# The drain of a graph-attention layer kernel: which engine sums x for the held blocks, and in what order the last blocks are normalised

## The chip, the cores and the metric

The kernel runs on one core of one Trainium2 chip. The metric is device microseconds of one launch of the program; less is better.

## The reference

```python
def gat(h, adj_mat, W, a):                       # 4 heads, 512 wide; h is x, 4096 x 512; adj_mat 4096 x 4096
    ht  = (h @ W).reshape(N, 4, 512).transpose(1, 0, 2)
    src = einsum('hnd,hd->hn', ht, a[:, :512, 0]); dst = einsum('hnd,hd->hn', ht, a[:, 512:, 0])
    e   = leaky_relu(src[:, :, None] + dst[:, None, :], 0.01) + adj_mat[None]
    att = softmax(e, axis=-1)
    return einsum('hij,hjd->hid', att, ht).mean(axis=0)

out = layernorm(x + gat(x, adj, W, a), axis=-1)   # eps 1e-5, no scale or shift; all float32
```

The entries of adj go up to 1e9, so that in nearly every row one entry is larger than the next by so much that the softmax is 1 at that entry and 0 elsewhere. The attention of such a row is the projected row of x at the column of the row's largest entry.

## The kernel before

The function `leading_rows` computes the whole output on the assumption that each softmax has one winner, and counts the rows for which a bound does not prove this. The function `general` computes softmax in full for blocks with such rows; with these inputs it is branched over.

**Blocks.** The 4096 rows are 32 blocks of 128 (NB = 32); row p of block ib is row 32p + ib of the matrix. The names used below are Q = 4, BEHIND = 24 and LATE = 28. Blocks 24 to 31 are called the held blocks here: the loop does not add x to them in the first place that it does for the others.

**The loop over t = 0 to 31.** In each turn SP issues the load of block t + 5 of adj (2 MB; in four pieces for block 0 and blocks 28 to 31), through the queue q1. VectorE takes maxima of segments of 64 entries (L158), then the largest segment of each row (`find_segment`, L165, L167). GpSimd fetches that segment anew by an indirect DMA (`lead`, L171). Two turns later VectorE finds the place within the segment (`find_column`, L193), and GpSimd fetches the row of x at that column (`y`, L181) by another indirect DMA (`gather_rows`). One turn after that TensorE transposes y (`turn`, L208), ScalarE copies it out as `yt` (L210), and TensorE multiplies it by the mean of the heads' weights (`products`, L221; a float32 matmul of 128x512 is two records in the profile). For blocks below 24 the row's own x is added in PSUM by a product with the identity (`residual`, L214). ScalarE then computes mean and variance in two passes (`stats`, L243, L245), GpSimd the reciprocal root (`rstd`, L248 to L250), and ScalarE the normalised rows in place of x (`finish`, L254). For blocks 24 to 27 ScalarE only puts the projected rows by (`put_by`, L234), because their x is not loaded yet.

**The order.** The instructions of each engine are issued in the order of the program text (`manual_schedule`); the framework adds semaphores for dependencies. What is later in the text on an engine cannot overtake what is earlier. SP's DMAs have eight completion semaphores that are used in turn, so SP issues a DMA only when the eighth one before it has landed.

**The drain** is the text from the last turn of the loop on. SP loads x of the held blocks, then stores the first 24 blocks. For row block 31 VectorE searches the column in the whole row of adj (`find_column_in_row`, L201), without the fetch of the segment. `row_norm` (L228) is needed for the bound; `bound`, `test`, `count` and `report` compute the number of unproved rows, and on TensorE they are the small products `px` (L362, L367, L386), which stand between the turns and products of blocks 29 to 31. In the kernel before:

- x is added to the put-by rows of blocks 24, 25 and 26 by GpSimd (`add_x`, L237), the first of them ahead of the last segment fetch, the second and third around the fetch of y of block 31; block 27 is summed on VectorE. Blocks 28 and 29 get x by `residual` on TensorE.
- the last of the four products of blocks 24 to 28 stands behind the next block's `turn`.
- `moments`, `factor` and `normalise` are the pieces of a second kind of normalising, by `bn_stats` on VectorE with a root on ScalarE (L274, L278, L280, L283, L290). They are spread over the text, so that a root is asked for before its result is used. Blocks 27 to 31 use it; blocks 27 and 31 use ScalarE for the last step as well (`finish`, L303).
- block 31 is projected in two halves of 256 columns (L259, L263), each with its own statistics (`stats_of_half`, L297); in `finish_in_halves` VectorE writes one half and ScalarE the other.

SP stores blocks 28, 29, 24 with 25, 30, 26 with 27, and 31 at the end (L306).

Of the kernel before, what the change touches and what calls it, by code (L numbers as in the profile page):

```python
# [9 lines left out]
F32 = mybir.dt.float32  # L10
# [56 lines left out]
def leading_rows(ctx, tc, x, adj, W, a, out, ident, v, n_bad, any_bad):  # L67
# [47 lines left out]
    def load_x(lo, n):  # L115
        nc.sync.dma_start(hold[:, ds(lo, n), :], x_rows[:, ds(lo, n), :])
# [69 lines left out]
    def find_inner(ib):  # L186
        nc.vector.max(out=inner[:, ib, :], in_=lead_of[ib])
# [16 lines left out]
    def turn(ib):  # L204
        y = y_t.pop(ib)
        tp = psum.tile([P, KB, P], F32, name="tp", bufs=2)
        for kb in range(KB):
            nc.tensor.transpose(tp[:, kb, :], y[:, ts(kb, P)], ident)  # L208
        yt = yt_of[ib] = rows.tile([P, KB, P], F32, name="yt")
        nc.scalar.copy(yt, tp)  # L210

    def residual(ib):
        o_ps[ib] = psum.tile([P, D], F32, name="o")
        nc.tensor.matmul(o_ps[ib], ident, hold[:, ib, :], start=True, stop=False)  # L214

    def products(ib, lo=0, hi=KB):
        start = ib not in o_ps
        if start:
            o_ps[ib] = psum.tile([P, D], F32, name="o")
        for kb in range(lo, hi):  # L220
            nc.tensor.matmul(  # L221
                o_ps[ib], yt_of[ib][:, kb, :], w_sum[:, kb, :],
                start=(start and kb == 0), stop=(kb == KB - 1),
            )

    def row_norm(ib):
        sq = rows.tile([P, D], F32, name="sq")
        nc.scalar.activation(sq, hold[:, ib, :], AF.Square, accum_out=xx[:, ib : ib + 1])  # L228
# [4 lines left out]
            o_ps["by"] = adj_pool.tile([P, N // D, D], F32, name="adj_t")  # L233
        nc.scalar.copy(o_ps["by"][:, ib - BEHIND, :], o_ps.pop(ib))  # L234

    def add_x(engine, ib):
        engine.tensor_add(hold[:, ib, :], hold[:, ib, :], o_ps["by"][:, ib - BEHIND, :])  # L237
        o_ps[ib] = hold[:, ib, :]

    def stats(ib):  # L240
        o, i = o_ps[ib], slice(ib, ib + 1)
        sq = rows.tile([P, D], F32, name="sq")
        nc.scalar.activation(sq, o, AF.Identity, scale=-1.0 / D, accum_out=nm[:, i])  # L243
        sq = rows.tile([P, D], F32, name="sq")
        nc.scalar.activation(sq, o, AF.Square, bias=nm[:, i], accum_out=sd[:, i])  # L245

    def rstd(i):
        nc.gpsimd.tensor_scalar(sd[:, i], sd[:, i], 1.0 / D, EPS, op0=OP.mult, op1=OP.add)  # L248
        nc.gpsimd.tensor_tensor(sd[:, i], sd[:, i], power[:, : i.stop - i.start], op=OP.pow)  # L249
        nc.gpsimd.tensor_mul(nm[:, i], nm[:, i], sd[:, i])  # L250

    def finish(ib):
        i = slice(ib, ib + 1)
        nc.scalar.activation(hold[:, ib, :], o_ps.pop(ib), AF.Identity, bias=nm[:, i], scale=sd[:, i])  # L254

    def residual_in_halves(ib):
        o_ps[ib] = [psum.tile([P, D // 2], F32, name="o") for _ in range(2)]
        for k, o in enumerate(o_ps[ib]):
            nc.tensor.matmul(o, ident, hold[:, ib, ts(k, D // 2)], start=True, stop=False)  # L259
# [5 lines left out]
                start=False, stop=(kb == KB - 1),  # L265
            )

    mean_var, rt = {}, {}

    def moments(ib):  # L270

        if ib < NB - 1:
            st = small.tile([P, nc.vector.BN_STATS_DIM], F32, name="st", bufs=2)
            nc.vector.bn_stats(st, o_ps[ib])  # L274
        else:
            st = halves_st
        mv = mean_var[ib] = small.tile([P, nc.vector.BN_AGGR_DIM], F32, name="mv", bufs=3)
        nc.vector.bn_aggr(mv, st)  # L278
        r = rt[ib] = sd[:, ib : ib + 1]
        nc.scalar.activation(r, mv[:, 1:2], AF.Sqrt, bias=eps)  # L280

    def factor(ib, shift=False):
        nc.vector.reciprocal(rt[ib], rt[ib])  # L283
        if shift:
            nc.vector.scalar_tensor_tensor(
                nm[:, ib : ib + 1], mean_var[ib][:, 0:1], -1.0, rt[ib], op0=OP.mult, op1=OP.mult
            )

    def normalise(ib, o, columns=slice(0, D)):
        nc.vector.tensor_scalar(  # L290
            hold[:, ib, columns], o, mean_var[ib][:, 0:1], rt[ib], op0=OP.subtract, op1=OP.mult
        )

    halves_st = once.tile([P, 2, nc.vector.BN_STATS_DIM], F32, name="halves_st")

    def stats_of_half(ib, k):
        nc.vector.bn_stats(halves_st[:, k, :], o_ps[ib][k])  # L297

    def finish_in_halves(ib):

        halves, i = o_ps.pop(ib), slice(ib, ib + 1)
        normalise(ib, halves[0], slice(0, D // 2))
        nc.scalar.activation(hold[:, ib, D // 2 :], halves[1], AF.Identity, bias=nm[:, i], scale=sd[:, i])  # L303

    def store(queue, lo, n):
        queue.dma_start(out_rows[:, ds(lo, n), :], hold[:, ds(lo, n), :])  # L306
# [93 lines left out]
    for t in range(NB):  # L400
        if t == NB // 2:
            tc.mark_branch_hint_location("general", engines=HINTED)
        if t in x_at:
            load_x(*x_at[t])
        load_adj(t + AHEAD)
        middle = 1 if t > LATE else 2
        segment_maxima(t, 0, middle)
        if t >= COLUMN:
            find_column(t - COLUMN)
        segment_maxima(t, middle, PIECES)  # L410
        pair = FINISH <= t < BEHIND + FINISH and t % 2 == 0
        if pair:
            rstd(slice(t - FINISH, t - FINISH + 2))
        if t == NB - 1:
            for ib in (BEHIND, LATE, BEHIND + 2, LATE + 2):
                load_x(ib, 2)
            row_norm(BEHIND)
            row_norm(BEHIND + 1)
            add_x(nc.gpsimd, BEHIND)
        find_segment(t)  # L420
        if t < 2:
            mean_of_heads(t)
        elif t == 2:
            mean_of_heads(2)
            mean_of_heads(3)
        if t == 0:
            turn_a()
        turned = [(*vectors[0], turn_w(*vectors.pop(0))) for _ in range(vectors_at.get(t, 0))]
        if t == 16:
            head_norms()  # L430
        ib = t - PROJECT
        if ib >= 0:
            turn(ib)
            if ib > BEHIND:
                products(ib - 1, KB - 1, KB)
            if ib < BEHIND or ib == LATE:
                residual(ib)
        for some in turned:
            head_vector(*some)
        if ib >= 0:  # L440
            products(ib, 0, KB if ib < BEHIND else KB - 1)
        if t >= BEHIND + STATS:
            put_by(t - STATS)
        elif t >= STATS:
            stats(t - STATS)
            row_norm(t - STATS)
        if pair:
            finish(t - FINISH)
            finish(t - FINISH + 1)

    row_norm(BEHIND + 2)
    row_norm(BEHIND + 3)
    row_norm(LATE)
    store(nc.sync, 0, Q)
    for ib in range(Q, BEHIND, 2):
        store(nc.sync, ib, 2)
    find_column(NB - 2)
    add_x(nc.gpsimd, BEHIND + 1)
    find_column_in_row(NB - 1)
    add_x(nc.gpsimd, BEHIND + 2)  # L460
    turn(NB - 3)
    products(NB - 4, KB - 1, KB)
    residual(NB - 3)
    products(NB - 3)
    for ib in range(LATE + 1, NB):
        row_norm(ib)
    stats(BEHIND)
    moments(LATE)
    bound(0)
    for ib in range(BEHIND, NB):  # L470
        find_inner(ib)
    factor(LATE)
    normalise(LATE, o_ps.pop(LATE))
    turn(NB - 2)
    residual_in_halves(NB - 1)
    products(NB - 2, 0, 1)
    bound(1)
    add_x(nc.vector, LATE - 1)
    stats(BEHIND + 1)
    moments(LATE - 1)  # L480
    products(NB - 2, 1, KB - 1)
    rstd(slice(BEHIND, BEHIND + 2))
    stats(BEHIND + 2)
    bound(2)
    test()
    pg = count()
    rstd(slice(BEHIND + 2, BEHIND + 3))
    moments(NB - 3)
    factor(LATE - 1, shift=True)
    report(pg)  # L490
    factor(NB - 3)
    normalise(NB - 3, o_ps.pop(NB - 3))
    turn(NB - 1)
    finish(BEHIND)
    finish(BEHIND + 1)
    products(NB - 2, KB - 1, KB)
    products_of_half(NB - 1, 0)
    products_of_half(NB - 1, 1)
    nc.vector.tensor_add(hold[:, NB - 2, :], o_ps[NB - 2], hold[:, NB - 2, :])
    o_ps[NB - 2] = hold[:, NB - 2, :]  # L500
    moments(NB - 2)
    stats_of_half(NB - 1, 0)
    factor(NB - 2)
    normalise(NB - 2, o_ps.pop(NB - 2))
    finish(BEHIND + 2)
    finish(BEHIND + 3)
    stats_of_half(NB - 1, 1)
    moments(NB - 1)
    factor(NB - 1, shift=True)
    finish_in_halves(NB - 1)  # L510
    for ib, n in ((NB - 4, 1), (NB - 3, 1), (BEHIND, 2), (NB - 2, 1), (BEHIND + 2, 2)):
        store(nc.sync, ib, n)
    store(nc.sync, NB - 1, 1)


# [151 lines left out]
```

## Time and profile before

| what | before |
|---|---|
| median of 6 runs | 242.73 us (242.31 to 243.97) |
| the profiled execution's own time | 243.38 us |
| its span in the profile | 241.8 us, so 1.58 us lie around it |
| busy: TensorE, VectorE, ScalarE, GpSimd | 198.9, 186.7, 111.6, 101.2 us |
| moved by DMA | 97.73 MB, 404 GB/s on average |
| granted TensorE clock | 0.966 on average |

Times in the texts are microseconds from the start of the span of the profiled execution. PE is TensorE, DVE is VectorE, ACT is ScalarE, POOL is GpSimd, SP is SyncE; a q behind one of these names marks its instruction queue. In a line of the timeline the columns are the start, the duration, the engine, the source line, the operation, the output and inputs, shapes and the count, and in brackets how long the engine had been idle and what released it. In the lines that cut the span into 40 slices each digit is the busy share in tenths.

### The profile page before, as it was taken

What the parts mean: (1) busy time and instruction counts of PE and PEld (TensorE: products, weight loads), DVE (VectorE), ACT (ScalarE), POOL (GpSimd) and SP (SyncE); (2) the same over time, 40 slices, a digit from 0 to 9 for tenths busy, and PEclk for the clock granted to TensorE, in tenths of its full rate; (3) what the DMA queues carried; (4) which work ended last, traced back from release to release, by engine and by line L of the source; (5) the groups of instructions that cost most, each with busy time, mean ns of one, the idle gap of its engine ahead of it and who ended that gap; (6) DMA issues with size and microseconds to landing.
All of it is one profiled execution on the core that took longest, in us unless ns stands there. A gap on an engine that the chain in (4) does not pass through costs nothing.

```text
span 241.8 us, 2519 instructions
## 1 busy us (share of the span) xinstructions
PE 198.9 (82%) x683; PEld 102.4 (42%) x683; DVE 186.7 (77%) x308; ACT 111.6 (46%) x267; POOL 101.2 (42%) x215
## 2 busy tenths in 40 slices
PE   0097849899999999999968789688886988979891
PEld 0034516645555555555523334233333433334460
DVE  2617864659959895999599987998699999978592
ACT  2001202115575757575756464646464455247572
POOL 1022232405626463546434643564264554566130
PEclk9999799679999999999999999999997999999997
DMA  6999999999999999999999999999999999999985
GB/s 228 419 424 420 428 419 424 413 423 411 425 415 417 407 423 420 421 412 416 429 415 417 420 415 420 422 407 418 412 424 404 399 400 401 400 414 419 413 333 215
DMA packets 14850, 97.73 MB, mean 404 GB/s; under 512 B 2281, under 2 KB 2281, under 8 KB 9969
## 3 DMA queue, kind: packets, MB, share of 16 engines
q1 hardware_dynamic: 11232, 88.09, 88.4%
q0 software_dynamic: 3584, 9.44, 10.0%
q8 instruction: 6, 0.10, 0.2%
q14 instruction: 12, 0.09, 0.1%
q10 hardware_dynamic: 16, 0.02, 0.0%
HBM read 89.15 MB, written 8.39 MB: 403 GB/s over the span
## 4 chain that ended last, share of the span: by engine, by line
issue 31%; POOL 30%; DMA 23%; PE 10%; ACT 1%; DVE 1%; SPq 1%; POOLq 1%; DVEq 0%
DMA hold<-in_x_dram 13%; POOL y L181 10%; POOL lead L171 10%; PE o L221 5%; DMA hold<-in_L_gnn_W_dram 4%; POOL sd L249 4%; DMA y<-in_x_dram,col 3%; DMA lead<-in_adj_dram,row 2%; POOL start L176 2%; POOL row L169 2%; POOL col L195 2%; PE o L263 1%; PE o L214 1%; POOL sd L248 1%; PE pv L335 1%
## 5 line engine op out<-in xcount | busy, mean ns | idle before, releaser
L158 DVE TENSOR_REDUCE seg<-adj_t 128x32 f32<-128x2048 f32 (+1 forms) x74 | 146.3, 1987 | 40.2 <-DMA adj_t<-in_adj_dram 39.9
L221 PE MATMUL o<-w_sum,yt 128*128 128x512 f32 x248 | 117.5, 614 | 0.7 <-ACT yt L210 0.7
L221 PEld LDWEIGHTS o<-w_sum,yt 128*128 128x128 f32 x248 | 45.5, 195 | 54.9 <-issue 43.8
L210 ACT COPY yt<-tp 128x512 f32<-128x512 f32 x32 | 18.8, 587 | 44.2 <-PE tp L208 37.7
L171 POOL DMA_INDIRECT lead<-in_adj_dram,row x32 | 32.3, 1010 | 14.0 <-POOL row L169 14.0
L181 POOL DMA_INDIRECT y<-in_x_dram,col x32 | 30.9, 965 | 16.1 <-POOL col L195 14.6
L311 PE MATMUL o<-hold,ident 128*128 128x512 f32 x32 | 18.4, 727 | 17.7 <-DMA hold<-in_L_gnn_W_dram 17.7
L208 PE MATMUL tp<-ident,y 128*128 128x128 f32 x128 | 19.7, 277 | 15.2 <-DMA y<-in_x_dram,col 15.2
L214 PE MATMUL o<-hold,ident 128*128 128x512 f32 x52 | 28.3, 628 | 1.1 <-DMA hold<-in_x_dram 1.1
L208 PEld LDWEIGHTS tp<-ident,y 128*128 128x128 f32 x128 | 14.3, 141 | 28.7 <-issue 27.2
L195 POOL TENSOR_TENSOR col<-start,within 128x1 uint32<-128x1 uint32 x31 | 5.9, 190 | 47.7 <-DVE within L193 47.7
L329 ACT COPY wt<-tp 128x512 f32<-128x512 f32 x16 | 9.2, 587 | 35.7 <-PE tp L327 35.7
L169 POOL TENSOR_TENSOR row<-at,first 128x1 uint32<-128x1 uint32 x32 | 6.1, 190 | 40.0 <-DVE at L167 40.0
L228 ACT ACTIVATE sq<-hold 128x512 f32<-128x512 f32 x32 | 19.8, 619 | 4.2 <-DMA hold<-in_x_dram 4.2
L335 PEld LDWEIGHTS pv<-at_d,wt 128*128 128x128 f32 x128 | 17.2, 200 | 7.4 <-ACT wt L329 3.7
L311 PEld LDWEIGHTS o<-hold,ident 128*128 128x128 f32 x32 | 7.2, 237 | 26.6 <-POOL row L169 12.7
L312 ACT ACTIVATE w_sum<-o 128x512 f32<-128x512 f32 x4 | 2.4, 598 | 33.5 <-PE o L311 33.5
L254 ACT ACTIVATE hold<-o,nm,sd 128x512 f32<-128x512 f32 x24 | 17.3, 771 | 0.0
L245 ACT ACTIVATE sq<-o,nm 128x512 f32<-128x512 f32 x24 | 16.5, 688 | 0.8
L335 PE MATMUL pv<-at_d,wt 128*128 128x2 f32 x128 | 16.0, 249 | 0.6 <-ACT wt L329 0.6
L243 ACT ACTIVATE sq<-o 128x512 f32<-128x512 f32 x24 | 14.6, 609 | 0.0
L327 PEld LDWEIGHTS tp<-ident,hold 128*128 128x128 f32 x64 | 7.9, 142 | 6.9 <-issue 6.9
(85 smaller groups left out, 137.5 us busy)
## 6 DMA issues: line engine op xcount, KB each, us to landing
adj_t<-in_adj_dram SPq DMA_DIRECT2D x27, 2048.0 KB
adj_t<-in_adj_dram SPq DMA_DIRECT2D x20, 512.0 KB
hold<-in_x_dram SPq DMA_DIRECT2D x6, 1024.0 KB
out_dram<-hold SPq DMA_DIRECT2D x12, 512.0 KB
hold<-in_L_gnn_W_dram SPq DMA_DIRECT2D x4, 1024.0 KB
hold<-in_x_dram SPq DMA_DIRECT2D x4, 512.0 KB
out_dram<-hold SPq DMA_DIRECT2D x1, 1024.0 KB
out_dram<-hold SPq DMA_DIRECT2D x4, 256.0 KB
```

The costliest lines, as they stand in the source:

```text
L158: nc.vector.tensor_reduce(seg_of[ib][:, ts(k, S // n)], adj_t[ib][:, ts(k, N // n)].rearrange("p (s e) -> p s e", e=E), axis=AX.X, op=OP.max,)
L171: nc.gpsimd.indirect_dma_start(out=lead, out_offset=None, in_=adj_segs, in_offset=bass.IndirectOffsetOnAxis(ap=row[:, :1], axis=0),)
L181: nc.gpsimd.indirect_dma_start(out=y, out_offset=None, in_=x, in_offset=bass.IndirectOffsetOnAxis(ap=col[:, :1], axis=0),)
L208: nc.tensor.transpose(tp[:, kb, :], y[:, ts(kb, P)], ident)
L210: nc.scalar.copy(yt, tp)
L214: nc.tensor.matmul(o_ps[ib], ident, hold[:, ib, :], start=True, stop=False)
L221: nc.tensor.matmul(o_ps[ib], yt_of[ib][:, kb, :], w_sum[:, kb, :], start=(start and kb == 0), stop=(kb == KB - 1),)
L228: nc.scalar.activation(sq, hold[:, ib, :], AF.Square, accum_out=xx[:, ib : ib + 1])
L245: nc.scalar.activation(sq, o, AF.Square, bias=nm[:, i], accum_out=sd[:, i])
L254: nc.scalar.activation(hold[:, ib, :], o_ps.pop(ib), AF.Identity, bias=nm[:, i], scale=sd[:, i])
L311: nc.tensor.matmul(o, ident, hold[:, w_at + kb * H + h, :], start=(h == 0), stop=(h == H - 1))
L335: nc.tensor.matmul(pv[:, kb, h : 2 * H : H], wt[:, k, :], at_d[:, k, h : 2 * H : H], start=(k == 0), stop=(k == KB - 1),)
```

## The change

Only the drain and the last turns of the loop differ.

- `add_x` is on VectorE for blocks 24 to 27, all of it behind the last search; GpSimd has no sum of x any more. The `residual` products of blocks 28 and 29 are gone; VectorE adds x to the projected rows of 28, 29 and 30 in the new `finish_last`.
- All four products of a block stand together again, behind the block's own turn; only the last product of block 29 stands behind the turn of block 30.
- `moments`, `factor` and `normalise` are gone. `finish_last` has the whole chain of a block in one place: sum, `bn_stats`, aggregate, root on ScalarE, reciprocal, normalise. Blocks 28, 29 and 30 go through it. Blocks 24 to 27 go through `stats` on ScalarE; 24 and 25 through `rstd` on GpSimd, 26 and 27 through the new `rstd_late`, on VectorE with a root on ScalarE, which stands behind `finish_last` of block 30.
- The four loads of x and the `row_norm` calls stand together behind the loop, in the order of the blocks. The eight `find_inner` stand behind the sums.
- `finish_in_halves` has the chain of block 31 in one place, behind `finish` of blocks 26 and 27; both halves are written by VectorE.

```diff
-    def add_x(engine, ib):
-        engine.tensor_add(hold[:, ib, :], hold[:, ib, :], o_ps["by"][:, ib - BEHIND, :])
+    def add_x(ib):
+        nc.vector.tensor_add(hold[:, ib, :], hold[:, ib, :], o_ps["by"][:, ib - BEHIND, :])
...
+    def rstd_late(i):
+        nc.vector.tensor_scalar(sd[:, i], sd[:, i], 1.0 / D, EPS, op0=OP.mult, op1=OP.add)
+        nc.scalar.activation(sd[:, i], sd[:, i], AF.Sqrt)
+        nc.vector.reciprocal(sd[:, i], sd[:, i])
+        nc.vector.tensor_mul(nm[:, i], nm[:, i], sd[:, i])
...
+    def finish_in_halves(ib):
+        halves = o_ps.pop(ib)
+        st = small.tile([P, 2, nc.vector.BN_STATS_DIM], F32, name="st2", bufs=1)
+        for k in range(2):
+            nc.vector.bn_stats(st[:, k, :], halves[k])
+        mv = small.tile([P, nc.vector.BN_AGGR_DIM], F32, name="mv", bufs=2)
+        nc.vector.bn_aggr(mv, st)
+        r = small.tile([P, 1], F32, name="r", bufs=2)
+        nc.scalar.activation(r, mv[:, 1:2], AF.Sqrt, bias=eps)
+        nc.vector.reciprocal(r, r)
+        for k in range(2):
+            nc.vector.tensor_scalar(
+                hold[:, ib, ts(k, D // 2)], halves[k], mv[:, 0:1], r, op0=OP.subtract, op1=OP.mult
+            )
+    def finish_last(ib, residual):
+        o = o_ps.pop(ib)
+        if residual:
+            nc.vector.tensor_add(hold[:, ib, :], o, hold[:, ib, :])
+            o = hold[:, ib, :]
...
+        nc.vector.bn_stats(st, o)
...
+        nc.vector.bn_aggr(mv, st)
...
+        nc.scalar.activation(r, mv[:, 1:2], AF.Sqrt, bias=eps)
+        nc.vector.reciprocal(r, r)
+        nc.vector.tensor_scalar(hold[:, ib, :], o, mv[:, 0:1], r, op0=OP.subtract, op1=OP.mult)
...
-        if t == NB - 1:
-            for ib in (BEHIND, LATE, BEHIND + 2, LATE + 2):
-                load_x(ib, 2)
-            row_norm(BEHIND)
-            row_norm(BEHIND + 1)
-            add_x(nc.gpsimd, BEHIND)
...
-            if ib > BEHIND:
-                products(ib - 1, KB - 1, KB)
-            if ib < BEHIND or ib == LATE:
+            if ib < BEHIND:
                 residual(ib)
...
-            products(ib, 0, KB if ib < BEHIND else KB - 1)
+            products(ib)
...
-    row_norm(BEHIND + 2)
-    row_norm(BEHIND + 3)
-    row_norm(LATE)
+    for ib in range(BEHIND, NB, 2):
+        load_x(ib, 2)
     store(nc.sync, 0, Q)
     for ib in range(Q, BEHIND, 2):
         store(nc.sync, ib, 2)
     find_column(NB - 2)
-    add_x(nc.gpsimd, BEHIND + 1)
     find_column_in_row(NB - 1)
-    add_x(nc.gpsimd, BEHIND + 2)
+    for ib in range(BEHIND, NB - 2):
+        row_norm(ib)
     turn(NB - 3)
-    products(NB - 4, KB - 1, KB)
-    residual(NB - 3)
-    products(NB - 3)
-    for ib in range(LATE + 1, NB):
+    for ib in range(NB - 2, NB):
         row_norm(ib)
-    stats(BEHIND)
-    moments(LATE)
+    products(NB - 3, 0, KB - 1)
+    finish_last(NB - 4, True)
     bound(0)
-    for ib in range(BEHIND, NB):
-        find_inner(ib)
-    factor(LATE)
-    normalise(LATE, o_ps.pop(LATE))
     turn(NB - 2)
+    add_x(BEHIND)
+    add_x(BEHIND + 1)
+    products(NB - 3, KB - 1, KB)
     residual_in_halves(NB - 1)
     products(NB - 2, 0, 1)
     bound(1)
-    add_x(nc.vector, LATE - 1)
+    products(NB - 2, 1, KB - 1)
+    add_x(BEHIND + 2)
+    add_x(BEHIND + 3)
+    stats(BEHIND)
     stats(BEHIND + 1)
-    moments(LATE - 1)
-    products(NB - 2, 1, KB - 1)
     rstd(slice(BEHIND, BEHIND + 2))
-    stats(BEHIND + 2)
+    for ib in range(BEHIND, NB):
+        find_inner(ib)
     bound(2)
     test()
     pg = count()
-    rstd(slice(BEHIND + 2, BEHIND + 3))
-    moments(NB - 3)
-    factor(LATE - 1, shift=True)
+    stats(BEHIND + 2)
+    turn(NB - 1)
+    finish_last(NB - 3, True)
     report(pg)
-    factor(NB - 3)
-    normalise(NB - 3, o_ps.pop(NB - 3))
-    turn(NB - 1)
     finish(BEHIND)
     finish(BEHIND + 1)
+    stats(BEHIND + 3)
     products(NB - 2, KB - 1, KB)
     products_of_half(NB - 1, 0)
     products_of_half(NB - 1, 1)
-    nc.vector.tensor_add(hold[:, NB - 2, :], o_ps[NB - 2], hold[:, NB - 2, :])
-    o_ps[NB - 2] = hold[:, NB - 2, :]
-    moments(NB - 2)
-    stats_of_half(NB - 1, 0)
-    factor(NB - 2)
-    normalise(NB - 2, o_ps.pop(NB - 2))
+    finish_last(NB - 2, True)
+    rstd_late(slice(BEHIND + 2, LATE))
     finish(BEHIND + 2)
     finish(BEHIND + 3)
-    stats_of_half(NB - 1, 1)
-    moments(NB - 1)
-    factor(NB - 1, shift=True)
-    finish_in_halves(NB - 1)
     for ib, n in ((NB - 4, 1), (NB - 3, 1), (BEHIND, 2), (NB - 2, 1), (BEHIND + 2, 2)):
         store(nc.sync, ib, n)
+    finish_in_halves(NB - 1)
     store(nc.sync, NB - 1, 1)
```

## The prediction

> **What bounds the kernel now.** First the page's slices: do the last microseconds hang on DMA, as the rest does?
>
> ```profile
> PE   0097849899999999999968789688886988979891
> DMA  6999999999999999999999999999999999999985
> GB/s 228 419 424 420 428 419 424 413 423 411 425 415 417 407 423 420 421 412 416 429 415 417 420 415 420 422 407 418 412 424 404 399 400 401 400 414 419 413 333 215
> ```
>
> A slice is 6.05 us. DMA is full up to 230 us; the loop before that is bound by bytes, which the change leaves alone. Only in the last two slices does DMA thin out, to 333 and 215 GB/s: there the stores wait for results. So I costed the drain, in order of time. The chain that ended last names its path:
>
> ```profile
> 218.48 8.02 DMA y<-in_x_dram,col
> 227.26 0.86 PE o L259 x4
> 228.13 0.94 PE o L221 x2
> 229.37 1.91 PE o L221 x4
> 232.02 0.86 PE o L221 x2
> 232.88 3.55 PE o L263 x16
> ```
>
> The end hangs on the rows y of block 30, whose gather GpSimd starts at 218.48, and then on TensorE without a gap. The timeline by engine shows what stands before that gather, and the hand-offs in the last 10 us:
>
> ```profile
> 215.19 1.27 POOL L237 TENSOR_TENSOR hold<-hold,adj_t 128x512 f32<-128x512 f32 x1 [1.62 <-ACT sq L228]
> 216.41 0.20 POOL L169 TENSOR_TENSOR row<-at,first 128x1 uint32<-128x1 uint32 x1
> ...
> 226.63 0.63 PE L208 MATMUL tp<-ident,y 128*128 128x128 f32 x4 [0.80 <-DMA y<-in_x_dram,col]
> ...
> 232.06 0.59 ACT L210 COPY yt<-tp 128x512 f32<-128x512 f32 x1 [0.18 <-PE tp L208]
> 232.54 1.52 ACT L254 ACTIVATE hold<-hold,nm,sd 128x512 f32<-128x512 f32 x2
> 234.64 0.29 ACT L280 ACTIVATE sd<-mv,eps 128x1 f32<-128x1 f32 x1 [0.59 <-DVE mv L278]
> 234.85 1.50 ACT L254 ACTIVATE hold<-hold,nm,sd 128x512 f32<-128x512 f32 x2
> 237.16 0.29 ACT L280 ACTIVATE sd<-mv,eps 128x1 f32<-128x1 f32 x1 [0.81 <-DVE mv L278]
> 237.88 0.56 ACT L303 ACTIVATE hold<-o,nm,sd 128x256 f32<-128x256 f32 x1 [0.43 <-DVE nm L285]
> ```
>
> See in it: GpSimd's sum of block 24 delays the row numbers of block 31 (216.41); turn 30 starts at 226.63; yt of block 31 ends at 232.65; ScalarE is done with blocks 26 and 27 at 236.35, while TensorE still multiplies (to 236.42), so the last root (237.16) finds it free. The last store is issued at 238.47; the span ends 3.37 later.
>
> I call T the start of turn 30 and Y the end of yt 31. Before: T = 226.63, Y = T + 6.02, last store = Y + 5.82.
>
> **Step 1, GpSimd loses three sums (L237, 1.27 us each): T.** Only the one at 215.19 stands before work that someone waits for. VectorE's segment index of block 31 is ready at 215.58, so the row numbers start at 215.66 instead of 216.41. The lead gather follows 0.7 after such a start where it had to wait for it (204.96 to 205.66, 210.31 to 211.01), so at 216.36, and lasts 0.97; start, col and the gather of y 30 follow as before, at 217.95 instead of 218.48: 0.53 earlier. Its last packet landed at 226.01, 7.5 after the issue, because one DMA engine was 1.5 us behind the others; y 29 and y 31 took 6.7 and 6.8. TensorE starts 0.6 after the landing. With 6.7 to 7.5, T is 225.25 to 226.05; with no gain at all, 226.63. A floor is set by TensorE's order: px (L362) stands before turn 30 and waits for xm, which now waits for all of block 28 on VectorE. From 221.48: sum 0.68, bn_stats 0.69, aggregate 0.18, root 0.29, reciprocal 0.15, normalise 0.55 (its source is now SBUF: 0.55 at 235.26, 0.81 from PSUM at 232.26), xm 0.19, and about 0.03 for each hand-off: 224.4, px done at 225.0. I take T = 225.8, 0.8 earlier: between the landings, nearer to block 30's own, since the other traffic is the same.
>
> **Step 2, TensorE.** Blocks 24 to 28 get their fourth product back before the next turn. TensorE then waits some 0.6 for yt in each of those turns of the loop, but it waits up to 3.0 us there anyway for the next y (the waits table: 15.2 us in 15 waits on y). Only the fourth product of block 29 is placed later, behind turn 30: two records at 0.43, **+0.86** between T and Y. The two residual products (L214) that go were ahead of T, in TensorE's slack: nothing. `count` waits for VectorE's test: the bound's px ends at T + 3.6, the test takes 1.3 (229.41 to 230.72), so T + 4.95; TensorE comes to it at T + 5.45. The eight `find_inner` (1.10) and four sums (0.67 each) end at 228.5, before the bound's px at 229.4. That cover is half a microsecond; beyond it every delay of VectorE counts in full. ScalarE's three `stats` (1.45 each, from 227.1) end at 231.5, and yt 31 is wanted at 232.1: covered by 0.6. So Y = T + 6.88.
>
> The sums on VectorE have two SBUF operands. In this trace GpSimd's sum at 219.47 lay inside VectorE's search of the whole row (4.42 us for 4096 elements), which shows no stall; no row has a VectorE sum beside a GpSimd gather. The new sums start at 224.3, behind the gather of y 31 (222.33 to 223.30), so I put nothing. In the Trainium skill, "SBUF — State Buffer", section "SBUF: two separate sides", VectorE work with two SBUF inputs and GpSimd share one port pair, and of the two "the other fully blocks". By that page a sum that met the gather would hold it for the length of the sum; y 31, landed at 229.13 and used at 231.37, could bear that, so the sum stays the same either way.
>
> **Step 3, the tail behind Y.** This is the large term. On ScalarE the text now has: root 29, finish 24, finish 25, stats 27, root 30, roots of 26 and 27, finish 26, finish 27, root 31. None can pass another. With row durations, counted from Y:
>
> - root 29 ends at 0.2; two finishes start 0.72 apart, from 0.1: free at 1.53; stats 27 takes 1.46: free at 2.99.
> - VectorE meanwhile: reciprocal and normalise of 29 (to 0.97), report (three operations, 0.37), sum, bn_stats and aggregate of 30 (to 2.89). Block 30 thus waits for block 29's root, which waits for yt 31; before, it was summed at 232.99, Y + 0.34, now at Y + 1.27.
> - root 30 2.99 to 3.28; reciprocal and normalise of 30 to 4.04; the scaling of 26 and 27 (0.2) to 4.15; their root to 4.46; reciprocal and product to 4.85.
> - finish 26 and 27 from 4.88, ScalarE free at 6.32. VectorE does both half statistics (0.43 each) and the aggregate to 5.9, so root 31 waits for ScalarE: 6.31 to 6.60. That is the new wait, 0.4, in place of none.
> - reciprocal to 6.79, two half normalises on VectorE one behind the other (0.54, pitch 0.47; before, one on each engine) to 7.80; the last store at 7.83.
>
> 7.83 against 5.82: **+2.01**. TensorE's halves end at Y + 3.77 as before, and no longer decide. Behind the last store I keep 3.37; the store of 26 with 27 stands 1.4 ahead of it instead of 2.1, which may add up to 0.4.
>
> The order of loads of x only swaps blocks 26, 27 with 28, 29; the later pair landed at 216.95, and is first used on VectorE after 221.4: nothing. Block 28's store waits for an earlier store until 225.74 in any case.
>
> **Sum.** T -0.8, product +0.86, tail +2.01: +2.07, say +2.1. The profiled execution took 243.38 (span 241.8 and 1.58 around it), so it would take 245.5. It lay 0.65 above the median of 242.73; on the median's footing the forecast is 244.8. A measurement of this kernel tells about 0.3% (0.73 us) from no change.
>
> **Rivals.**
>
> - *The gather moves, the landing does not.* The straggling DMA engine served other queued traffic until 226.0, whenever the request came. T stays at 226.63: 0.86 + 2.01 = +2.9, 245.6. For it: block 30 alone had so late a last packet. Against: y 29 and y 31 landed at one distance from their issue.
> - *T at its floor.* No straggler: T = 225.0 to 225.1, -1.55; +1.3, 244.0. For it: 6.7 us is the commoner landing, and 217.95 + 6.7 + 0.6 is 225.25, all but the floor.
> - *Half clock in the drain.* The page's clock row has slices at 0.6 to 0.7; in the drain all was at full clock until TensorE was done. A stretch of 3.4 us at half clock (its length earlier in the trace) between T and Y adds 1.7: 246.5.
> - *Not slower: the gather is worth more than the tail costs.* Place: block 30's y. The leads, 32 KB each against 256 KB, landed 5.0 to 5.3 after issue; at 5.2 y 30 would be there at 223.15 and T at 223.8, -2.85, which pays for 2.87: 242.7. It decides from T below 224.5 on. Against it: all three late gathers took 6.7 or more, and px would have to come before 225.0, against the 2.9 us chain of block 28.
>
> **How the numbers follow.** Forecast 0.50; landing unmoved 0.22; floor 0.15; half clock 0.06; not slower 0.05, half of it beyond the bound; 0.02 for what I have not seen. Faster 0.03, same 0.04, slower 0.93. The range takes the floor case at 244.0 less 0.2, and the unmoved landing at 245.6 with 0.4 of colliding stores and 0.2 of spread: 243.8 to 246.2. Half clock and the not-slower case stay out.
>
> **What would show it.** Right: in the changed profile the gather of y 30 starts near 217.95; Y lies near 232.7, and the last root starts at once behind the second finish of 26 and 27, near Y + 6.3, with VectorE idle before its reciprocal; the last store about 7.8 behind Y. Wrong: turn 30 released by px instead of the DMA (floor); `count` waiting for VectorE (step 2's cover gone); root 31 not behind the finishes, or a last store less than 7 behind Y (step 3 too large).

## The result, and the profile after

The changed kernel takes 243.88 us in the median of 20 runs (242.91 to 245.32), the kernel before 242.59 in 43. The ratio is 1.0048, 95% interval 1.0035 to 1.0062: slower by 1.2 us (0.8 to 1.5). The forecast was slower by 2.1. The profiled execution took 245.11, span 243.5; a stretch at half the TensorE clock, told of below, is part of what sets it above the median.

The page's slices of the kernel after:

```profile
PE   0199959999999999999969779499959888869970
PEclk9999779999999999999999999889988999995996
DMA  6999999999999999999999999999999999999953
GB/s 246 438 425 408 427 433 409 437 417 424 412 425 422 404 433 423 425 405 432 422 422 412 425 424 421 416 425 423 422 421 398 408 406 407 404 418 417 392 194 136
```

Two things differ from the page before. DMA thins out earlier and lower (194 and 136 GB/s in the last two slices), so the stores wait longer for results. And the slices of the loop are a little higher: the second to the thirtieth move 421.8 GB/s on average, before 418.5, though the prediction left the loop alone. The chain that ended last, in order of time:

```profile
209.47 8.41 DMA y<-in_x_dram,col
...
219.51 5.49 PE o L221 x6
...
231.25 0.59 ACT yt L210
232.03 1.41 ACT hold L261 x2
...
234.08 0.81 ACT sq L245 x2
...
236.66 1.39 ACT hold L261 x2
...
238.09 0.29 ACT r L283
```

Before, TensorE's products were the last long piece; now the chain goes through ScalarE behind yt 31, as step 3 had it. The hand-offs themselves, from the timeline of GpSimd, TensorE and ScalarE of the kernel after:

```profile
212.54 0.19 POOL L169 TENSOR_TENSOR row<-at,first 128x1 uint32<-128x1 uint32 x1 [2.11 <-DVE at L167]
214.82 0.96 POOL L181 DMA_INDIRECT y<-in_x_dram,col  x1 [0.27 <-POOL col L195]
...
225.01 0.67 PE L208 MATMUL tp<-ident,y 128*128 128x128 f32 x4
...
231.25 0.59 ACT L210 COPY yt<-tp 128x512 f32<-128x512 f32 x1 [0.48 <-PE tp L208]
231.74 0.30 ACT L301 ACTIVATE r<-mv,eps 128x1 f32<-128x1 f32 x1
231.93 1.51 ACT L261 ACTIVATE hold<-hold,nm,sd 128x512 f32<-128x512 f32 x2
...
236.66 1.52 ACT L261 ACTIVATE hold<-hold,nm,sd 128x512 f32<-128x512 f32 x2 [0.43 <-DVE nm L257]
238.09 0.28 ACT L283 ACTIVATE r<-mv,eps 128x1 f32<-128x1 f32 x1
```

Turn 30 starts at T = 225.01 and yt 31 ends at Y = 231.84, so Y = T + 6.83 (forecast 6.88; before 6.01). Root 31 has no idle time in front of it: it comes straight behind finish 27. The last store is issued at 239.62, Y + 7.78 (forecast 7.83; before 5.83). Both terms, +0.82 and +1.95, are as they were sized. They hold in the other profiles too: the 15 kernels of this document that keep the order of the kernel before from turn 30 on have Y = T + 5.98 to 6.01 and the last store at Y + 5.83; the changed kernel and its two padded forms (after_y32, after_all256) have 6.76 to 6.83 and 7.78 to 7.79. The rest of the sum cannot be right, since these two alone make 2.8.

Where it went is in the start of the drain. VectorE has block 31's index at 212.46 in this profile, 3.1 us earlier than the 215.58 before; the first row is the kernel before, the second the kernel after:

```profile
215.36 0.22 DVE L167 FIND_INDEX8 at<-top,seg 128x8 uint32<-128x64 f32 x1
...
212.24 0.22 DVE L167 FIND_INDEX8 at<-top,seg 128x8 uint32<-128x64 f32 x1
```

Against that, this execution lost time in the drain: six matmuls (L221, 219.51) took 5.49, at a granted clock of 0.51 between 218.2 and 225.1, where the same six took 2.84 in the profile of after_y32 below.

### The profile page after: what moved, and what is told of

Same layout as the page of the kernel before. It is cut to its first block, busy times and chain, and to the rows that moved or that the text cites. A ratio compares the mean times of both kernels' runs of the same rounds, so it can differ in the third digit from the quotient of the medians.

```text
span 243.5 us, 2509 instructions
## 1 busy us (share of the span) xinstructions
PE 200.8 (82%) x679; PEld 103.3 (42%) x679; DVE 189.1 (78%) x312; ACT 112.1 (46%) x270; POOL 95.9 (39%) x209
## 4 chain that ended last, share of the span: by engine, by line
issue 27%; POOL 24%; DMA 22%; PE 19%; DVE 3%; ACT 3%; SPq 1%; POOLq 0%; DVEq 0%; ACTq 0%
DMA adj_t<-in_adj_dram 15%; PE o L221 11%; POOL lead L171 8%; POOL y L181 8%; DMA y<-in_x_dram,col 7%; POOL sd L249 2%; PE o L214 2%; PE tp L208 2%; PE pv L335 2%; DVE seg L158 2%; POOL start L176 2%; POOL col L195 2%; POOL row L169 2%; ACT hold L261 1%; PE tp L327 1%
## 5 line engine op out<-in xcount | busy, mean ns | idle before, releaser
L221 PE MATMUL o<-w_sum,yt 128*128 128x512 f32 x248 | 119.3, 623 | 4.2 <-ACT yt L210 4.2
L221 PEld LDWEIGHTS o<-w_sum,yt 128*128 128x128 f32 x248 | 46.4, 197 | 59.7 <-issue 46.2
L208 PEld LDWEIGHTS tp<-ident,y 128*128 128x128 f32 x128 | 14.8, 142 | 25.1 <-issue 24.0
L335 PEld LDWEIGHTS pv<-at_d,wt 128*128 128x128 f32 x128 | 16.3, 191 | 6.8 <-ACT wt L329 3.5
L311 PEld LDWEIGHTS o<-hold,ident 128*128 128x128 f32 x32 | 8.1, 265 | 25.4 <-POOL row L169 11.1
L335 PE MATMUL pv<-at_d,wt 128*128 128x2 f32 x128 | 15.3, 244 | 0.6 <-ACT wt L329 0.6
```

Of the source, the lines that this page charges most:

```text
L221: nc.tensor.matmul(o_ps[ib], yt_of[ib][:, kb, :], w_sum[:, kb, :], start=(start and kb == 0), stop=(kb == KB - 1),)
L311: nc.tensor.matmul(o, ident, hold[:, w_at + kb * H + h, :], start=(h == 0), stop=(h == H - 1))
L335: nc.tensor.matmul(pv[:, kb, h : 2 * H : H], wt[:, k, :], at_d[:, k, h : 2 * H : H], start=(k == 0), stop=(k == KB - 1),)
```

## The experiments

They ask two things: what each step of the drain costs alone, and why the loop is faster. `before` is the kernel before in every ratio.

**The place of the tiles.** The programs differ in one more way than the drain. Dropping `halves_st` and one buffer of `mv`, and adding `r` and `st2`, moves the pool of wt, y, yt and sq by 32 bytes in each partition of SBUF: y begins 32 bytes short of a multiple of 256 before, at a multiple after. The adj tiles move as well: the paddings that bring them to a multiple, 224 bytes in before_all256 and 288 in after_all256, put them 32 past one before and 224 past one after. No run measures that second move alone.

```diff
+    pad = small.tile([P, 8], F32, name="pad", bufs=1)     # after_y32, before_y0; 24 columns in before_rows64
+    nc.gpsimd.memset(pad, 0.0)
```

> The changed kernel with 32 bytes of padding ahead of the tiles y, so that they begin at 32 bytes past a multiple of 64, as in the kernel before; in the changed kernel they begin at a multiple of 64. Theory A (only the drain matters; where tiles lie does not): as the changed kernel, 243.9 us within 0.4, and the last search (L201) starts as early as in the changed kernel's profile, near 213.6. Theory B (the tiles' place sets the rate of the DMA stream through the whole loop): 1.3 us or more slower, 245.2 us or above, with the last search near 216 to 217.

244.86, ratio 1.0090 (1.0072 to 1.0108); index of block 31 at 214.78. 32 bytes of padding make the changed kernel 1.0 us slower (0.5 to 1.6): more than theory A allows, less than theory B asked for.

> The kernel before with 32 bytes of padding ahead of the tiles y, so that they begin at a multiple of 64 as in the changed kernel. Theory A: as the kernel before, 242.6 us within 0.4, last search near 217. Theory B: 1.3 us or more faster, 241.3 us or below, with the last search near 214 to 215.5.

240.89, ratio 0.9950 (0.9935 to 0.9966); index at 212.53. The same padding makes the kernel before 1.2 us faster by the ratio (0.8 to 1.6). The direction is that of theory B both ways, and theory A is out; the size is at the lower end of what B asked for, or below. Which tile, and which multiple, the following runs ask.

```diff
-        y = y_t[ib] = rows.tile([P, D], F32, name="y", bufs=4)
+        y = rows.tile([P, D + 16], F32, name="y", bufs=4)[:, ds(8, D)]     # D + 64 in the ..256 kernels
+        y_t[ib] = y
```

> The kernel before with each tile y widened by 64 bytes and used from its 32nd byte on, so that only the rows that the gather writes begin at a multiple of 64; yt, sq and wt stay 32 bytes past one. Theory B1 (it is the DMA's writes of y): as the kernel with 32 bytes of padding, 240.9 to 241.5 us, the index of block 31 found near 212.5. Theory B2 (it is what TensorE and ScalarE read or write in the tiles behind y): as the kernel before, 242.5, index found near 215.

242.17, ratio 0.9985 (0.9975 to 0.9995), index at 214.41: neither theory, a small gain.

> The kernel before with the adj tiles at a multiple of 64 instead of 32 bytes past one, and y left where it was. Theory C1 (any DMA write that begins off a multiple of 64 costs the stream, by its number of pieces): adj is written in pieces of up to 16 KB against y's 2 KB, so its 64 MB have as many piece beginnings as 8 MB of y, and the gain is about as for y, 1 us or more, 241.5 or below. Theory C2 (only the gather's queue suffers): no change, 242.5.

242.36, ratio 0.9993 (0.9976 to 1.0011): no change. These paddings bring adj to 64 past a multiple of 256 and y from 224 to 32 past one.

> The kernel before with 32 bytes of padding ahead of all large tiles: hold, w_sum, adj_t, lead, y and yt all begin at a multiple of 64. C1: gains of y and adj add up, and loads of W and x and the stores gain too: 239.5 to 240.5. C2: as with y alone, 240.9 to 241.5.

241.03, ratio 0.9939 (0.9922 to 0.9955): as with y's pool alone.

> The kernel before with each tile sq (ScalarE's scratch output) widened by 64 bytes and used from its 32nd byte on, so that ScalarE's writes of it begin at a multiple of 64; y, yt, wt as before. If sq carries the effect of the padding: 241.0 to 241.5 us and the index of block 31 near 212.5. If it is yt and wt, or y: 242.5 within 0.3.

242.64, ratio 1.0005 (0.9996 to 1.0015).

> The same for yt and wt alone, which ScalarE writes and TensorE loads as weights. If they carry the effect: 241.0 to 241.5. If sq or y: 242.5 within 0.3.

242.57, ratio 1.0013 (1.0002 to 1.0024).

> All tiles of that pool (sq, yt, wt, y) used from their 32nd byte on, while the tiles' own beginnings, and seg and lead ahead of them, stay where they were. If the effect of the padding is where these tiles' data begin, whichever of them: 240.9 to 241.4, as with the padding. If it comes from something else that the padding moved: 242.2 as with y alone.

242.34, ratio 0.9999 (0.9982 to 1.0015). So it looked as if the padding had moved something else. But 64 bytes of widening put only one of y's four buffers at a multiple of 256, and before_only_y0 had gained some 0.4 us of the 1.2 that the padding gave. So the multiple was tried:

> The kernel before with 96 bytes of padding ahead of the small tiles: y, yt, wt and sq begin at 64 past a multiple of 256 (32 bytes of padding put them at a multiple of 256; without it they are 32 short of one). If a multiple of 64 is what counts: 241.0 to 241.4. If it has to be 256 (or 128): 242.5 within 0.3.

242.51, ratio 1.0002 (0.9984 to 1.0019): a multiple of 64 is not enough.

> The kernel before with the tiles y widened by 256 bytes and used from their 32nd byte on: y's data begin at a multiple of 256 in all four buffers (with 64 bytes of widening only in one of four), the rest stays. If y's place modulo 256 carries the effect: 240.9 to 241.4, block 31's index near 212.5. If not: 242.2 to 242.5.

240.88, ratio 0.9941 (0.9918 to 0.9965), index at 212.46. It is the rows that the gather writes; of the places tried, only a multiple of 256 helps (32, 64 and 224 past one do not; 128 past one was not tried).

> The same widening by 256 bytes for y, yt, wt and sq: the data of all four begin at a multiple of 256, while the tiles ahead of them stay where they were. If the place of these data modulo 256 is the cause, whichever of them: 240.9 to 241.4. If it is something else that the padding moved (segments, leads, indices): 242.2 to 242.5.

240.61, ratio 0.9915 (0.9899 to 0.9932): y and the rest of its pool, with all other tiles in place. By the intervals it is not clear of y alone.

> The kernel before with adj_t alone at a multiple of 256; hold, y and the rest at their old places modulo 256. If the gains of y and adj are separate and add up: about 3 us of the 4.8 that all tiles gave, 239 to 240. If hold carries the rest: 241.5 or above.

240.08, ratio 0.9919 (0.9891 to 0.9948): adj alone gives 2.0 us (1.3 to 2.6), between what the two theories asked for.

> The kernel before with padding that brings hold, adj_t, y, yt, wt and sq all to a multiple of 256. If a multiple of 256 matters for every DMA write: below the 240.9 of the padded kernel, 239.5 to 240.4. If only the pool of y counts: 240.9 to 241.2.

237.74, ratio 0.9793 (0.9774 to 0.9812): 2.1% faster than the kernel before, below both kernels and below the range expected. The edit is three paddings (24 columns in `keep`, 32 in `once`, 16 in `small`). Adj and y account for 1.4 of the 2.1 points by their own runs; the rest was not split.

The stretches show it in the loop: of each line the columns are the stretch, busy times by engine, PE's clock, the DMA share and, last, GB/s. First the kernel before, then after, after_y32 and before_all256:

```profile
100.00:150.00 50.00, 44.80 (x154) 22.18 (x152) 42.17 (x70) 28.82 (x69) 23.90 (x52) 1.00 1.01 418
```

```profile
100.00:150.00 50.00, 43.65 (x143) 20.84 (x144) 42.61 (x70) 28.70 (x69) 24.17 (x53) 1.00 1.01 422
```

```profile
100.00:150.00 50.00, 44.35 (x157) 22.21 (x155) 42.45 (x69) 29.25 (x70) 24.18 (x50) 1.00 1.01 417
```

```profile
100.00:150.00 50.00, 44.52 (x141) 21.42 (x142) 43.24 (x70) 28.42 (x69) 24.70 (x53) 0.97 1.01 426
```

The DMA share is the same, full, in all four: what changes is how much a full stream moves. The order holds in the profiles of all twenty kernels. This stretch moves 417 to 419 GB/s where y and adj are off the multiple (or y is on it in one buffer of four), 421 to 422 with y on it, 423 with adj on it and 426 with all of them.

**The drain alone, at equal places.**

> The changed kernel with padding that brings hold, adj_t, y, yt, wt and sq to multiples of 256, to stand against the kernel before with the same (237.74). If the drain costs what the prediction's sum said and only the tiles' places hid it: 2.1 to 2.8 above, 239.8 to 240.5. If the drain is cheap by itself: 239 or below.

240.24 against 237.74, ratios 0.9903 (0.9881 to 0.9925) against 0.9793: by their quotient 1.011, some 2.7 us, with the two intervals taken together 1.9 to 3.4. In its profile Y = T + 6.76 and the last store Y + 7.79. after_y32 says the same against the kernel before, both with y off the multiple: 2.2 us (1.7 to 2.6). The profile of after_all256 has a stretch at half clock of its own ahead of T (granted clock 0.51 from 212.0 to 215.4): eight products of a block take 5.40 us where the eight of the block before took 3.70, and turn 29 follows without idle time.

```profile
205.08 3.70 PE L227 MATMUL o<-w_sum,yt 128*128 128x512 f32 x8 [0.73 <-ACT yt L216]
...
211.43 5.40 PE L227 MATMUL o<-w_sum,yt 128*128 128x512 f32 x8 [0.73 <-ACT yt L216]
216.67 0.60 PE L214 MATMUL tp<-ident,y 128*128 128x128 f32 x4
```

**Step 3 alone.** The kernel before up to `count`, then the tail of the changed kernel:

```diff
     pg = count()
-    rstd(slice(BEHIND + 2, BEHIND + 3))
-    moments(NB - 3)
...
+    stats(BEHIND + 2)
+    turn(NB - 1)
+    finish_last(NB - 3, False)
...
+    halves_at_once(NB - 1)      # finish_in_halves of the changed kernel
     store(nc.sync, NB - 1, 1)
```

> The kernel before up to the product px of count, and from there on the tail of the changed kernel (root 29 behind yt 31, finish 24 and 25, stats 27, root 30, roots of 26 and 27, finish 26 and 27, root 31, both halves on VectorE). Step 3 of the prediction alone: the last store 7.8 us behind the end of yt 31 instead of 5.8, and 2.0 to 2.5 us in time, 244.6 to 245.1. Rival (the tail was sized too large, which is why the whole change measured only 1.2): 243.8 or less.

245.25, ratio 1.0109 (1.0090 to 1.0128): 2.6 us. ScalarE's timeline of this kernel has Y = 230.70 and the same row:

```profile
230.11 0.59 ACT L210 COPY yt<-tp 128x512 f32<-128x512 f32 x1 [1.16 <-PE tp L208]
230.59 0.30 ACT L323 ACTIVATE r<-mv,eps 128x1 f32<-128x1 f32 x1
...
235.78 1.52 ACT L254 ACTIVATE hold<-hold,nm,sd 128x512 f32<-128x512 f32 x2 [0.43 <-DVE nm L310]
237.20 0.28 ACT L335 ACTIVATE r<-mv,eps 128x1 f32<-128x1 f32 x1
```

The last root starts 6.50 behind Y, the last store is issued at 238.74, Y + 8.04. The tail costs what was forecast, at its upper end; the interval is 2.2 to 3.1 us. (Block 29 is normalised from PSUM here, in 0.81 us at 231.12, against 0.55 in the changed kernel, which is as much as 8.04 exceeds 7.78.)

**Step 2's product alone.**

```diff
-    products(NB - 3, 0, KB - 1)
+    products(NB - 3)
...
     add_x(BEHIND + 1)
-    products(NB - 3, KB - 1, KB)
```

> The changed kernel with the fourth product of block 29 back ahead of turn 30. Step 2 of the prediction: 0.86 between the start of turn 30 and the end of yt 31 goes (6.8 to 6.0), while turn 30 itself is not later as it waits for block 30's rows: 243.0 against 243.9. Rival (turn 30 waits for the px of the bound, which the product now delays by the same 0.86): no change, 243.9.

242.66, ratio 1.0004 (0.9982 to 1.0027) against the changed kernel's 1.0048: 1.1 us (0.4 to 1.7), Y = T + 6.16 in place of 6.76 to 6.83. The rival's "no change" is out by the time. But in this one profile turn 30 does come straight behind px, at 223.34 behind 223.23, as the rival had it, so the 1.1 is not accounted for row by row.

**Step 1 alone.**

```diff
-            add_x(nc.gpsimd, BEHIND)
         find_segment(t)
...
     find_column(NB - 2)
+    add_x(nc.gpsimd, BEHIND)
     add_x(nc.gpsimd, BEHIND + 1)
```

> The kernel before with GpSimd's sum of block 24 moved behind the gather of y of block 30; nothing else. Step 1 of the prediction: the gather starts 0.5 us earlier against the end of the index search of block 31 (2.4 us behind it instead of 2.9), turn 30 follows, and the time falls by 0.5 (to 242.1); if the late last packet goes as well, by up to 1.5 (241.1). Rival (the landing does not move with the issue): 242.6, no change.

242.32, ratio 0.9995 (0.9982 to 1.0008): no change. The gather did start 2.37 behind the index, but TensorE's row, in the timeline of this kernel, had no use for it:

```profile
219.27 0.63 PE L208 MATMUL tp<-ident,y 128*128 128x128 f32 x4
...
224.89 0.27 PE L362 MATMUL px<-ident,xm 128*1 128x128 f32 x1
225.00 0.60 PE L208 MATMUL tp<-ident,y 128*128 128x128 f32 x4
```

The rows of block 30 had landed at 223.36. Turn 30 comes straight behind px, and px behind the products of block 29: TensorE's own row sets T. In the profile before, y 30 landed 7.5 behind its issue, here 5.8. Of the profiles of the kernel before and the 15 kernels made from it, 12 have turn 30 straight behind px; those of the kernel before, before_adj0, before_yt0 and before_adj256 wait 0.5 to 0.8 for y 30.

> The kernel before with the 32 bytes of padding, and with the fourth product of block 28 and the residual of block 29 ahead of turn 29, where TensorE waits for y 29 anyway. Theory (TensorE's own row from turn 29 to px sets the start of turn 30, so what is taken out of it moves the end): 0.8 to 1.7 off the 240.9 of the padded kernel, 239.2 to 240.1, until y 30 decides. Rival (the landing of y 30 sets it, as step 1 had it): 240.9, no change.

240.94, ratio 0.9943 (0.9922 to 0.9963), against 240.89 with the padding alone: no change. Turn 29 went from 216.83 to 218.14 in the profiles and turn 30 from 222.53 to 223.09: there was no idle time ahead of turn 29, the two products only changed sides. It agrees with a TensorE row that is full up to px, but does not show what shortening it would bring.

## Why the prediction was right or wrong

- *What bounds the kernel now.* "the loop before that is bound by bytes, which the change leaves alone" is the step that failed. The bytes stayed; the rate did not. The place of y in SBUF followed from sizes of statistics tiles in the drain, and it was worth 1.0 (after_y32) to 1.4 us (before_only_y256), with 418 GB/s in the loop off the multiple and 422 on it. No term and no rival had it.
- *Step 1, T 0.8 earlier.* No run shows this gain. The gather moved as worked out (0.54 earlier against the index), but gather_first gained 0.1 within an interval of -0.4 to +0.2. T was read from a late execution. Eight kernels have y off the multiple (two of them with one buffer of four on it) and the order of the kernel before up to turn 30; in their profiles T lies at 224.1 to 226.6, 225.5 in the median, and the 226.63 of the prediction is the latest. The changed kernel with y off the multiple (after_y32) has 225.32, so the forecast place of T, 225.8, was near, and the 0.8 was the distance to an untypical start. In five of the eight TensorE's own row sets T, so the rival in which the landing does not move came near in its result, but not by its reason, a straggling DMA engine. after_all256 can't add to this: its T, 9.84 behind block 31's index against 9.71 in before_all256, has the half-clock stretch in it. The rows of block 30 had landed there at 219.61 and TensorE starts some 0.6 behind a landing, so without the stretch its T of 220.73 could have been 0.5 earlier at most. In after_y32, whose row on TensorE is shorter, turn 30 does wait for y 30:

```profile
223.29 0.27 PE L364 MATMUL px<-ident,xm 128*1 128x128 f32 x1 [0.29 <-DVE xm L362]
225.32 0.63 PE L210 MATMUL tp<-ident,y 128*128 128x128 f32 x4 [1.76 <-DMA y<-in_x_dram,col]
```

- *Step 2, +0.86.* Right: 0.82 in the trace, 1.1 (0.4 to 1.7) by after_prod_first. The cover for `count` held: its px comes at 230.41 in the profile after, without idle time behind the products. That the two dropped residuals cost nothing ahead of T was argued from slack; in gather_first's profile there is none between turn 29 and turn 30, in that of after_y32 turn 30 waits 1.76 for y 30. What they are worth was not measured alone.
- *Step 3, +2.01.* Right: 1.95 in the trace, 2.6 by before_new_tail. The new wait, root 31 behind the two finishes, stands where it was put.
- *The sum.* 0.82 + 1.95 + 0 = 2.8 for the drain, measured 2.2 and 2.7 at equal places; less 1.0 to 1.4 for y leaves 1.4 to 1.8 against the measured 1.2 (0.8 to 1.5). The last few tenths are not accounted for. That the forecast of 2.1 is no further off is in part luck: it counted a gain of 0.8 that did not come, and a gain of 1.0 to 1.4 came that it did not count.
- *The half-clock rival* did occur in the profiled execution: a stretch at half clock from 218.3 to 225.1, twice as long as the rival's 3.4, made six matmuls 2.6 us longer. It followed 2.1 us in which TensorE waited for y 29. The Trainium skill, "TensorE: Matmul & The Clock Gate", Part 1, ties half clock to an idle window of about 3.4 us. This trace does not show that rule: the wait was shorter, and in before_y0 TensorE waited 2.49 us ahead of its turn at 212.07 and no half clock followed in the drain. The runs hint that the changed kernel has such stretches more often: its granted clock, averaged over a run, is 0.955 or less in 9 of 22 runs, that of the kernel before in 8 of the 106 runs taken beside the experiments. Those nine runs have a median of 244.1 us, the other thirteen 243.7. An average does not say where in the run the stretch lay, and what in the order would bring it was not tried.

## What to carry to other kernels

A change that touches only the end of a kernel can move the rate of its whole stream, if it changes the size of any tile: compare the addresses of the large DMA targets in both programs, and the GB/s of a stretch that the change doesn't touch, before costing the rest. Read the wait that a step is to shorten in more than one profile; here the start that was to come earlier was the latest of eight. On an engine that works in order, a small operation placed behind two long ones is charged with what is left of both: here a root of 0.28 us came straight behind two finishes of 1.5 us together, 0.5 behind the statistics that it needed.

## What the runs showed of the hardware that was not expected

DMA writes into SBUF ran faster here when the data of each partition began at a multiple of 256 bytes. With y 224 past such a multiple (the kernel before, 242.59), 32 past one (before_adj0, 242.36) and 64 past one (before_rows64, 242.51) there was no difference clear of the intervals. In the traces the adj packets of 16 KB took 626 ns on average in the kernel before, 620 with y alone at a multiple, and 613 with all tiles there. So the place of y changed the time of adj's packets too; the packets of the leads (2 KB), whose place was not moved, stayed at 84.7 and 84.6.

The Trainium skill, "DMA: Bandwidth & Descriptors", section "How a descriptor splits into AXI transactions", says that a transaction must start at an address that is a multiple of 256; it words this for reads, and here it is the written side that moved. By that page a 2 KB row off a multiple takes nine transactions instead of eight, a 16 KB row 65 instead of 64. As an estimate from that count, 1/64 of the time of 64 MB at the 418 GB/s measured (160 us) is 2.5 us for adj, where before_adj256 gained 2.0; 1/8 of the time of y's 8 MB (20 us) is 2.5 us for y, where before_only_y256 gained 1.4. The page also counts the bytes ahead of the start as lost, which would make 224 past a multiple dearer than 32; no run here shows that. So the count has the right direction and about the size for adj, and too much for y; that it is the cause is not shown.
